# Moving every second block's h from row to time order with VectorE turns and SBUF copies, in a state-space kernel on Trainium2

## The chip, the cores and the metric

The kernel runs on one core of a Trainium2 chip, as one launch. The metric is device time in microseconds (us) from start to end of the launch. Engines are named as in the profile: PE is TensorE, DVE is VectorE, ACT is ScalarE, POOL is GpSimd, SP is SyncE, whose queue issues all of this kernel's transfers.

## What is computed

The input x has 1024 tokens of 512 values. It is normalized by rows (xn), and the output is x plus two branches of xn. Cut to what matters:

```
# branch 1: a state-space layer, here 128 heads of 64, 8 groups, state size 128, chunks of 128 tokens
gate, hBC, dt = split(xn @ in_proj_w.T)            # 8192, 10240 and 128 columns
hBC = silu(causal_conv4(hBC))                      # h: 8192, B: 1024, C: 1024 columns
dt  = clip(softplus(dt + dt_bias), 0, 100);  A_cum = cumsum over a chunk of dt * -exp(A_log)
xch = h * dt                                       # per head and token
Y_diag = (C B^T * exp(segsum)) @ xch               # inside a chunk
states = B^T (decay * xch), carried over chunks    # across chunks
Y = Y_diag + (C @ previous state) * exp(A_cum) + h * D
out1 = groupnorm(Y * silu(gate)) * norm_w @ out_proj_w.T
# branch 2: xn @ base_W.T plus low-rank experts, top 2 of 8 by a router
```

## The kernel before

**Tiles.** Channels are cut into blocks of 128. A block of h holds two heads: 128 channels in the partitions, 1024 tokens along the row. There are 64 h blocks, 64 gate blocks, 8 blocks of B and 8 of C (one per group). The eight chunks are called z. Float32 products are made from a high and a low part of each operand, three matmuls in place of one.

**One block** (`block`, from L729). Its weights are loaded (wr), split into high and low parts by ACT and POOL (L391, L392), multiplied on PE in two halves of 512 tokens (pp_r, L491), and taken out of PSUM: a gate block by one ACT operation per half (L743), an h, B or C block by ACT (L750) and three DVE taps of the convolution (L759), then one silu on ACT (L762).

**One step of the scan** (`scan`) handles two h blocks, so four heads; there are 32 steps, u = 0 to 31. Four mask tiles L are loaded as broadcast rows of acum_d and made into exp(-relu(.)) by ACT (L840, L842), and multiplied by the group's C B^T on DVE (L844). Then h, which has channels in its partitions, must get tokens into its partitions: PE transposes it chunk by chunk into PSUM (L818, eight 128x128 transposes per block, in two sets of four), and DVE multiplies each set by dt on its way out (xdt, L867). POOL weights xdt by the decay (xf, L873) and takes the low part (L880); PE makes chunk states from it (ps, L891), DVE carries them (st, L898 and L902). PE makes the two parts of the output (yo, L926, and y, L937, both 64 columns at a time, in halves of the array), DVE and POOL add and gate them (L929, L941, L944, L947), and the block is stored to g_d. A loop over groups with the output projection follows (po, L1010).

**The group's B** needs the same exchange. For it `turn` exists: DVE transposes all 32x32 squares of the block in one instruction (L779), which puts the right values into squares that stand in the wrong partitions; four stores (L778) write them to a DRAM buffer turn_d in another order, and one load (MB) brings them back. ACT and DVE then split B into high and low parts (L798, L800). A constant, TURNED, says whether blocks of h take this way too: with 0, as here, none does (`aside` is then false), with 2 every second one.

**The order.** Nothing is issued in the order in which it is written. Every operation is recorded with an engine, an assumed duration, the buffers it reads and writes, and an urgency (the table URGE, plus a shift per step and kind in SHIFT). A planner then plays the five engines forward in time and, whenever an engine is free, takes the ready operation with the lowest urgency, within limits on buffers of each kind (CAPS) and a charge for changing between kinds of matmul (TURN) or activation tables. The result is one fixed list of instructions per engine. Each engine works through its own list in order; an instruction that waits holds up all behind it on the same engine, SP's transfers included.

Of the kernel before, what the change touches and what calls it, by code (L numbers as in the profile page):

```python
# [49 lines left out]
URGE = dict(w=13.332, part=1.468, proj=-0.321, evac=-1.263, silu=-2.207, group=-1.454, hT=0.733, xdt=4.109,  # L50
            xf=-2.187, split=-0.021, ps=-5.287, st=-1.748, Ll=-4.271, Lr=7.668, Le=-0.828, Lm=10.124, el=-2.727,
            yo=-1.239, tt=-8.284, y=2.439, yt=-5.971, out=3.035, switch=3.602, c0=52.272, c=0.059, ffn=33.567,
            rt=-6.333, la=-1.718, early=-6.258, hold=0.271, gate=0.323, w0=100.494, SL=0.902, SH=0.088, SM=-4.419,
            LS=-0.037, LH=-0.076, LM=0.521, HS=3.572, HL=3.045, HM=-4.925, MS=-0.425, ML=-0.865, MH=0.797,
            hold2=-0.366, late=0.054, late2=0.096)
CAPS = dict(hs=5, gate=12, ct=2, L=7, e=3, xdt=9, turned=8, moved=3, wr=3, wh=9, wl=3, y=3, tt=2, xf=2, mm=16, ts=11, yy=8)

SHIFT = {}
for what, rows in dict(
        Le={1: 0.47, 2: -0.26, 3: -1.05, 4: -0.15, 5: 2, 6: -0.49, 7: 0.27, 9: -0.05, 12: -1.87, 13: 1.14, 14: 0.19,  # L60
            15: 0.82, 16: 0.61, 17: 0.64, 18: 0.12, 19: 1.35, 20: -0.65, 21: 0.59, 22: 0.59, 23: 0.11, 24: 0.26,
            26: 3.27, 27: 0.06, 28: 0.68, 29: -0.13, 30: 0.62, 31: 2.11},
        Ll={0: -0.81, 1: 1.29, 2: -0.45, 3: -0.27, 4: 0.34, 5: 1.51, 6: 0.55, 8: -0.1, 9: -3.54, 10: 0.17, 13: -2.75,
            14: 0.07, 15: 1.23, 16: -0.51, 19: 0.31, 21: 1.11, 23: 0.35, 24: -0.27, 26: -1.24, 27: -0.09, 28: 0.23,
            29: 1.87, 30: 2.91, 31: 1.26},
        Lm={1: -0.01, 3: 0.04, 4: -3.35, 5: 0.23, 6: 0.13, 8: -0.27, 9: 2.6, 10: -1.27, 11: 0.6, 15: -0.14, 16: 1.77,
            17: -0.48, 18: -3, 19: 0.19, 21: 0.05, 22: 0.04, 24: -0.04, 25: -1.05, 26: 0.09, 27: -1.02, 29: 2.34,
            30: -0.67},
        Lr={0: -0.03, 5: -0.35, 6: 0.1, 7: 0.58, 8: 0.8, 9: 0.35, 10: 0.01, 11: 0.64, 12: -0.05, 13: 0.15, 14: -0.03,
            15: 0.13, 17: -0.16, 18: 0.47, 19: -0.38, 22: -0.94, 23: 0.63, 25: 0.03, 26: 0.42, 27: 0.08, 28: 0.06,  # L70
            30: 0.07},
        el={0: -0.13, 1: -0.13, 4: 0.19, 8: 0.01, 9: -0.05, 10: 0.85, 11: -0.34, 12: 0.69, 13: 1.01, 17: 1.18,
            21: -0.42, 23: -0.65, 24: -0.88, 26: -0.39, 27: 0.31, 28: -0.01, 29: -0.41, 30: -0.51, 31: -1.96},
        gate={1: -0.11, 2: 0.17, 4: -2.2, 7: 0.08, 8: 0.03, 9: -0.25, 10: -0.2, 11: 0.88, 12: 0.1, 13: 0.52,
            15: -1.48, 17: 0.24, 18: -0.36, 20: -0.68, 21: -0.62, 22: -0.12, 24: -0.17, 25: -0.55, 26: 0.1,
            27: -0.59, 28: 1.26, 30: -0.35, 31: 0.23},
        group={0: 0.08, 2: -0.39, 3: 0.43, 5: -2.97, 6: 1.03, 7: -2.93, 10: -0.48, 11: 0.11, 12: -0.47, 13: -0.13,
            15: -1.26, 16: 0.08, 17: 0.15, 18: -0.31, 19: 0.47, 20: 0.01, 21: 0.14, 22: -1.25, 23: -0.61, 24: 0.03,
            25: -1.26, 26: 0.04, 27: -0.01, 28: -0.98, 29: 1.81, 30: -0.02},
        h={0: 0.22, 2: -0.03, 3: 0.11, 4: -0.06, 5: 0.19, 7: 0.02, 8: -0.07, 11: 0.48, 12: 0.22, 15: 0.26, 16: 0.32,  # L80
            18: -0.06, 20: -0.81, 21: 0.45, 22: -0.08, 24: -0.07, 25: -0.04, 27: 0.79, 28: 0.3, 29: 0.32, 31: 0.34},
        hT={0: 0.48, 1: 0.55, 3: -0.04, 4: 0.37, 6: -0.13, 8: 0.36, 9: 0.02, 10: -0.05, 11: 0.01, 12: -0.06,
            13: 0.21, 14: -0.11, 17: -4.33, 18: 0.18, 20: -2.06, 21: -1.02, 22: -0.17, 23: -0.65, 24: -0.09,
            25: 0.12, 28: 0.23, 30: -0.09, 31: -0.09},
        out={0: 0.06, 1: 0.58, 2: -0.1, 3: -0.33, 4: 0.66, 5: -0.97, 6: 0.57, 9: -0.06, 10: -0.56, 11: -0.59,
            12: -0.03, 13: -0.36, 14: 0.66, 15: 0.02, 16: 3.94, 18: 0.13, 19: 0.24, 22: 2.65, 23: -0.26, 24: 0.58,
            25: 0.09, 26: -0.03, 27: 0.6, 28: 0.8, 30: 0.18, 31: 0.82},
        ps={0: -0.19, 1: 0.04, 2: -0.24, 3: -0.19, 4: -2.42, 5: -0.69, 7: 4.13, 8: -0.01, 9: 0.27, 10: 0.44,
            12: 1.55, 14: -0.11, 16: -0.83, 19: 0.38, 20: -0.04, 22: 0.86, 25: -0.16, 28: -0.18, 30: 0.94, 31: -0.26},
        split={0: 0.69, 1: 2.29, 3: -0.09, 4: -0.05, 5: -1.39, 7: -1.51, 8: 0.12, 9: -0.12, 10: -0.34, 11: 0.11,  # L90
            12: 3.76, 14: -0.07, 15: 1.18, 17: -0.36, 18: 0.76, 20: -0.21, 21: 0.97, 22: -0.02, 23: -0.1, 24: -0.72,
            25: 1.26, 26: 1.68, 27: 0.02, 28: -0.28, 30: 0.66, 31: -0.4},
        st={0: -0.77, 2: -0.11, 3: 2.97, 4: 0.09, 5: -1.75, 6: 1.37, 8: -0.2, 9: -0.16, 10: -0.19, 11: -1.63,
            12: -0.01, 13: 0.17, 17: -2.04, 21: -1.34, 22: -0.12, 23: -0.74, 24: 0.82, 25: 1.04, 26: 0.02, 27: 0.28,
            28: -0.04, 29: 0.76, 30: -5},
        tt={0: 0.8, 1: 0.82, 2: 1.2, 3: -0.51, 4: -0.89, 5: 0.08, 6: -0.29, 7: -0.12, 8: 0.03, 10: -2.95, 11: 0.49,
            12: 0.35, 13: 1.11, 14: 0.25, 15: -0.03, 16: 0.52, 18: 1.56, 21: 0.03, 22: 0.7, 23: -0.66, 24: 1.74,
            26: 0.42, 27: -1.68, 28: 0.86, 31: -0.69},
        xdt={1: 0.04, 2: 0.59, 3: -0.11, 4: -1.62, 6: 0.48, 7: -0.02, 10: 0.28, 11: 0.12, 12: 0.65, 14: 0.23,
            15: -0.14, 16: 0.62, 17: -0.88, 18: -0.44, 19: -0.92, 20: -0.18, 21: -0.39, 22: -0.44, 25: -0.4,  # L100
            27: -0.96, 28: -3.62, 30: -0.03},
        xf={0: 0.18, 1: 0.11, 2: 0.25, 3: 1.29, 4: -0.1, 5: 0.65, 6: -0.05, 7: 0.52, 10: -0.16, 11: -0.98, 12: -1.46,
            13: -0.66, 14: 1.03, 15: -1.06, 16: 0.12, 18: 1.8, 19: -0.08, 20: -0.27, 21: 0.04, 22: -0.14, 23: -0.26,
            24: -1.59, 25: -0.15, 26: 0.23, 28: -1.22, 30: 0.35},
        y={0: 0.4, 1: -0.78, 2: -0.58, 3: 0.78, 4: 0.26, 5: -2.28, 8: -0.51, 9: -0.08, 10: 0.01, 11: -0.93,
            12: -0.05, 13: 0.37, 15: -0.75, 16: -0.1, 17: 0.35, 18: -0.03, 19: 0.2, 21: -0.65, 22: -0.16, 24: -0.73,
            26: -0.01, 27: -0.2, 28: -0.1, 30: 0.15, 31: 0.17},
        yo={0: -0.42, 1: -0.12, 2: -0.02, 5: 0.15, 6: -0.84, 10: 0.52, 11: 0.52, 12: -0.34, 13: 0.23, 15: -0.73,
            16: 0.52, 17: 0.33, 18: -0.6, 19: -1.53, 20: 1.18, 23: 0.02, 25: 1, 27: -0.46, 31: 0.02},
        yt={0: -1.42, 1: 0.96, 3: -1.19, 5: 0.1, 6: -0.03, 7: 0.63, 8: -0.17, 9: -0.63, 10: -1.86, 11: -0.23,  # L110
            12: -0.77, 13: 0.99, 14: -0.18, 17: -0.08, 18: 1.77, 19: 0.17, 20: -2.08, 22: 1.6, 25: -2.21, 26: 0.48,
            28: -0.7, 30: -1.5, 31: -0.01}).items():
    SHIFT |= {(u, what): by for u, by in rows.items()}
LAND = 1.15
TURNED = 0
# [186 lines left out]
def block_kernel(ctx, tc, x, in_w, conv_w, conv_b, dt_bias, A_log, Dv, norm_w, out_w,  # L302
# [31 lines left out]
    turn_d = [dram.tile([4, 32, 4, 256], F32, name=f"turn_d{i}") for i in range(4)]  # L334
# [27 lines left out]
    def thing(name):  # L362
        return pl.buf(None, name)
# [19 lines left out]
    TURN_D = [thing(f"turn_d{i}") for i in range(4)]  # L383
# [387 lines left out]
    def turn(src, name, at, urge):  # L771


        turned, moved = new("turned", f"T{name}"), new("moved", f"M{name}")

        def store():
            for q in range(4):
                sp.dma_start(turn_d[at][q].rearrange("r i f -> i r f"), turned()[:, 256 * q:256 * q + 256])  # L778
        op("DVE", 1.17, lambda: dve.transpose(  # L779
            turned().rearrange("p (q z c) -> p z q c", q=4, z=NZ), src().rearrange("p (z q r) -> p z q r", q=4, z=NZ)),  # L780
            r=[src], w=[turned], urge=urge)
        op("SP", 2.3, store, lag=LAND * 9.4, r=[turned], w=[TURN_D[at]], urge=urge)
        dma(lambda: moved().rearrange("p (i f) -> p i f", i=4), lambda: turn_d[at].rearrange("q r i f -> (q r) i f"),
            4.4, r=[TURN_D[at]], w=[moved], urge=urge)
        return moved
# [35 lines left out]
    def scan(u, hs, gate):  # L821
        g, gr = u // 4, groups[u // 4]

        def at(what):
            return u + URGE[what] + SHIFT.get((u, what), 0.0)
# [274 lines left out]
```

## Time and profile before

| what | value |
| --- | --- |
| median of 3 runs | 1593.33 us (1593.29 to 1593.93) |
| the profiled execution | 1591.37 us |
| its span, first to last instruction | 1589.6 us |
| transposes of h on PE (L818) | x512, 62.8 us busy, 272 ns each (median) |
| multiplication by dt on DVE (L867) | x128, 84.0 us busy, 682 ns mean |
| turns of B on DVE (L779) | x8, 9.9 us busy, 1239 ns mean |
| stores of turned B (L778) | x32, 128 KB each; loads of it x8, 512 KB each |
| ACT table loads | 109.1 (L842), 59.0 (L743) and 55.2 us (L762) |
| transfers on the SP queue | 236.76 MB, 48.7% of the 16 engines' span |

A profile row names the line, engine, operation, output and inputs, then count, busy time, mean duration of one, and the engine's idle time just before such instructions with what ended it. Matmuls overlap in the array, so the mean duration of one is longer than the distance between two starts. A row of the timeline has the start and length in us. A row of waits says which instruction waited for which, us in total, how often, and the longest.

### The profile page before, as it was taken

What the parts mean: (1) busy time and instruction counts of PE and PEld (TensorE: products, weight loads), DVE (VectorE), ACT (ScalarE), POOL (GpSimd) and SP (SyncE); (2) the same over time, 40 slices, a digit from 0 to 9 for tenths busy, and PEclk for the clock granted to TensorE, in tenths of its full rate; (3) what the DMA queues carried; (4) which work ended last, traced back from release to release, by engine and by line L of the source; (5) the groups of instructions that cost most, each with busy time, mean ns of one, the idle gap of its engine ahead of it and who ended that gap; (6) DMA issues with size and microseconds to landing.
All of it is one profiled execution on the core that took longest, in us unless ns stands there. A gap on an engine that the chain in (4) does not pass through costs nothing.

```text
span 1589.6 us, 28731 instructions
## 1 busy us (share of the span) xinstructions
PE 1579.8 (99%) x10498; PEld 1341.6 (84%) x10498; DVE 1311.4 (82%) x2237; ACT 1265.0 (80%) x2244; POOL 853.5 (54%) x768
## 2 busy tenths in 40 slices
PE   9999999999999999999999999999999999999999
PEld 8888888888888888888888888888877888888887
DVE  7799788887887969977978887888778888989785
ACT  6999988997989899997998998989883555545432
POOL 3288578676766875877767756869665000000000
PEclk9999999999999999999999999999999999999999
DMA  4636346543465354363453543644635556545532
GB/s 133 233 104 213 112 138 204 170 159 122 146 177 155 131 187 150 124 183 117 153 166 126 187 154 126 182 161 143 174 108 181 146 146 173 146 121 153 140 88 72
DMA packets 156061, 238.59 MB, mean 150 GB/s; under 512 B 21392, under 2 KB 91152, under 8 KB 155920
## 3 DMA queue, kind: packets, MB, share of 16 engines
q1 hardware_dynamic: 155920, 236.76, 48.7%
q8 instruction: 83, 1.36, 0.4%
q14 instruction: 58, 0.48, 0.1%
HBM read 195.70 MB, written 41.01 MB: 149 GB/s over the span
## 4 chain that ended last, share of the span: by engine, by line
PE 84%; ACT 10%; DMA 2%; issue 1%; DVE 1%; POOL 1%; SPq 0%; ACTq 0%; POOLq 0%
PE pp_r L491 39%; PE po L1010 22%; PE y L937 6%; PE yo L926 6%; PE ps L891 4%; PE hT L818 3%; ACT L L840 3%; PE pf L717 1%; ACT L842 1%; ACT L L842 1%; ACT L743 1%; ACT g L743 1%; PE cb L810 1%; ACT wh L391 1%; DMA e<-exp_d 1%
## 5 line engine op out<-in xcount | busy, mean ns | idle before, releaser
L491 PE MATMUL pp_r<-xh,wh 128*128 128x512 f32 x1144 | 454.5, 397 | 0.0
L491 PE MATMUL pp_r<-xl,wh 128*128 128x512 f32 x1144 | 446.6, 390 | 0.0
L491 PE MATMUL pp_r<-xh,wl 128*128 128x512 f32 x1144 | 446.3, 390 | 0.3 <-POOL wl L392 0.3
L759 DVE SCALAR_TENSOR_TENSOR h<-pp_r,cw,h 128x512 f32<-128x512 f32 (+2 forms) x384 | 283.0, 746 | 50.7 <-ACT h L750 45.6
L840 ACT ACTIVATE L<-L,As 128x128 f32<-128x128 f32 x1024 | 318.6, 391 | 1.2 <-DMA L<-acum_d 1.2
L392 POOL TENSOR_TENSOR wl<-wr,wh 128x512 fp32r<-128x512 f32 x144 | 196.2, 1369 | 177.1 <-ACT wh L391 120.5
L844 DVE TENSOR_TENSOR L<-L,cbm 128x1024 f32<-128x1024 f32 x128 | 202.9, 1596 | 64.3 <-ACT L L842 63.1
L491 PEld LDWEIGHTS pp_r<-xh,wh 128*128 128x128 f32 x1144 | 214.9, 188 | 47.8 <-issue 5.3
L491 PEld LDWEIGHTS pp_r<-xh,wl 128*128 128x128 f32 x1144 | 214.7, 188 | 47.3 <-POOL wl L392 1.1
L491 PEld LDWEIGHTS pp_r<-xl,wh 128*128 128x128 f32 x1144 | 215.1, 188 | 40.8
L944 POOL TENSOR_TENSOR yt<-yt,tt 128x384 f32<-128x384 f32 (+1 forms) x128 | 166.3, 1308 | 78.5 <-DVE yt L941 67.1
L1000 ACT ACTIVATE gr<-gr 128x1024 f32<-128x1024 f32 x64 | 67.9, 1061 | 150.3 <-DVE gl L998 149.4
L947 POOL TENSOR_TENSOR g<-yt,g 128x512 f32<-128x512 f32 x128 | 181.8, 1427 | 1.9
L880 POOL TENSOR_TENSOR xdl<-xf,xdh 128x512 fp32r<-128x512 f32 (+1 forms) x128 | 161.3, 1268 | 34.0 <-ACT xdh L878 33.0
L902 DVE SCALAR_TENSOR_TENSOR st<-st,eA,ps 128x64 f32<-128x64 f32 x768 | 156.0, 275 | 2.3 <-PE ps L891 1.2
L873 POOL TENSOR_TENSOR xf<-xdt,dec 128x512 f32<-128x512 f32 (+1 forms) x128 | 135.0, 1063 | 38.0 <-DVE xdt L867 31.7
L1001 DVE TENSOR_REDUCE sq<-gr 128x128 f32<-128x1024 f32 x64 | 128.3, 2010 | 21.4 <-ACT gr L1000 21.4
L842 ACT ACTIVATE L<-L 128x1024 f32<-128x1024 f32 x128 | 135.4, 1058 | 1.3
L1010 PE MATMUL po<-owh,gh 128*128 128x512 f32 x512 | 127.2, 391 | 0.0
L1010 PE MATMUL po<-owh,gl 128*128 128x512 f32 x512 | 126.7, 389 | 0.0
L1010 PE MATMUL po<-owl,gh 128*128 128x512 f32 x512 | 126.5, 389 | 0.0
L937 PE MATMUL y<-L,xdt 128*64 128x128 f32 x2048 | 122.7, 273 | 0.0
(178 smaller groups left out, 2706.4 us busy)
## 6 DMA issues: line engine op xcount, KB each, us to landing
L<-acum_d SPq DMA_DIRECT2D x128, 512.0 KB
wr<-in_w SPq DMA_DIRECT2D x144, 256.0 KB
g_d<-g SPq DMA_DIRECT2D x64, 512.0 KB
gr<-g_d SPq DMA_DIRECT2D x64, 512.0 KB
e<-exp_d SPq DMA_DIRECT2D x128, 224.0 KB
ow<-out_w SPq DMA_DIRECT2D x64, 256.0 KB
turn_d<-TB SPq DMA_DIRECT2D x32, 128.0 KB
MB<-turn_d SPq DMA_DIRECT2D x8, 512.0 KB
```

What stands on the lines that cost most here:

```text
L392: op("POOL", dur[1], lambda: pool.tensor_tensor(lo(), raw(), f32(hi()), ALU.subtract), r=[raw, hi], w=[lo], urge=urge, port=True)
L491: pe.matmul(acc(), a[:, k, :], b[:, k, halves(half)], start=n == 0, stop=n == 11)
L759: dve.scalar_tensor_tensor(d, acc()[:, :n], cw[:, ci, k:k + 1], d, ALU.mult, ALU.add)
L840: act.activation(L()[:, z, :], L()[:, z, :], AF.Relu, bias=As()[:, z, h:h + 1], scale=-1.0)
L842: op("ACT", 0.97, lambda L=L: act.activation(L(), L(), AF.Exp, scale=-1.0), w=[L], urge=at("Le") + 0.05 * a, table="exp")
L844: op("DVE", 1.14, lambda L=L: dve.tensor_tensor(L(), L(), gr.cbm(), ALU.mult), r=[gr.cbm], w=[L], urge=at("Lm") + 0.05 * a, port=True)
L880: op("POOL", 1.24 if n == 4 else 0.96, lambda xf=xf, zs=zs, cols=cols: pool.tensor_tensor(xdl()[:, zs, cols], xf(), f32(xdh()[:, zs, cols] ...
L902: dve.scalar_tensor_tensor(st()[:, z, c], st()[:, z - 1, c], eA()[:, 4 * u + a, z:z + 1], pt()[:, z % 2, c], ALU.mult, ALU.add)
L937: pe.matmul(yp()[64 * a:64 * a + 64, zsl(z4)], xdt[j]()[:, z, 64 * a:64 * a + 64], M[2 * j + a]()[:, z, :], start=True, stop=True)
L944: op("POOL", 1.25 if n == 4 else 0.97, lambda yt=yt, tt=tt, part=part: pool.tensor_tensor(yt()[:, part], yt()[:, part], tt()[:, part], ALU ...
L947: op("POOL", 1.24, lambda yt=yt, j=j, hf=hf: pool.tensor_tensor(gate[j]()[:, halves(hf)], yt(), gate[j]()[:, halves(hf)], ALU.mult), r=[yt ...
L1010: pe.matmul(po(), a()[:, b, :], wts[g, b // per][k]()[:, b % per, :], start=n == 0, stop=n == 23)
```

## The change

Three things change.

- TURNED goes from 0 to 2: of the two h blocks in each step, the second no longer goes through PE. In its place stand one DVE turn, 16 transfers, and two DVE multiplications by dt that read SBUF (one per head, all eight chunks at once).
- `turn` no longer goes through DRAM. The turned block is copied straight from SBUF to SBUF, square column by square column: 16 transfers of 32 partitions x 256 elements (32 KB), recorded as four operations of four. B's blocks take this way too.
- URGE, CAPS and SHIFT get new values throughout, so all five lists of instructions differ.

```diff
-CAPS = dict(hs=5, gate=12, ct=2, L=7, e=3, xdt=9, turned=8, moved=3, wr=3, wh=9, wl=3, y=3, tt=2, xf=2, mm=16, ts=11, yy=8)
+CAPS = dict(hs=5, gate=22, ct=2, L=7, e=2, xdt=15, turned=6, moved=6, wr=3, wh=4, wl=19, y=7, tt=3, xf=2, mm=37, ts=14, yy=12)
...
-TURNED = 0
+TURNED = 2
...
-    def turn(src, name, at, urge):
+    def turn(src, name, urge):
...
-        def store():
-            for q in range(4):
-                sp.dma_start(turn_d[at][q].rearrange("r i f -> i r f"), turned()[:, 256 * q:256 * q + 256])
         op("DVE", 1.17, lambda: dve.transpose(
             turned().rearrange("p (q z c) -> p z q c", q=4, z=NZ), src().rearrange("p (z q r) -> p z q r", q=4, z=NZ)),
             r=[src], w=[turned], urge=urge)
-        op("SP", 2.3, store, lag=LAND * 9.4, r=[turned], w=[TURN_D[at]], urge=urge)
-        dma(lambda: moved().rearrange("p (i f) -> p i f", i=4), lambda: turn_d[at].rearrange("q r i f -> (q r) i f"),
-            4.4, r=[TURN_D[at]], w=[moved], urge=urge)
+        for q in range(4):
+            def move(q=q):
+                for i in range(4):
+                    sp.dma_start(moved()[32 * q:32 * q + 32, 256 * i:256 * i + 256],
+                                 turned()[32 * i:32 * i + 32, 256 * q:256 * q + 256])
+            op("SP", 1.85, move, lag=LAND * 4.9, r=[turned], w=[(moved, 1 << q)], urge=urge)
         return moved
...
-        moved = turn(gr.B, f"B{g}", g % 4, urge)
+        moved = turn(gr.B, f"B{g}", urge)
...
             if aside:
-                moved = turn(hs[j], f"h{b}", b % 4, at("hT"))
+                moved = turn(hs[j], f"h{b}", at("hT"))
```

The multiplication that a turned block takes is in the kernel before already, behind `if aside`: for each of the two heads it reads the moved tile and dt, and writes all eight chunks of that head's half of xdt.

## The prediction

> **What bounds the kernel now.** I read the page's first, second and fourth parts, then the busy times of one stage, then TensorE's own waits, then the timeline around one set of transposes.
>
> ```profile
> span 1589.6 us, 28731 instructions
> ...
> PE 1579.8 (99%) x10498; PEld 1341.6 (84%) x10498; DVE 1311.4 (82%) x2237; ACT 1265.0 (80%) x2244; POOL 853.5 (54%) x768
> ...
> PEclk9999999999999999999999999999999999999999
> ...
> PE 84%; ACT 10%; DMA 2%; issue 1%; DVE 1%; POOL 1%; SPq 0%; ACTq 0%; POOLq 0%
> ```
>
> TensorE is busy for all but 9.8 us of the span, at a clock that is granted in full, and the chain that ends last runs 84% through it. The h transposes stand almost wholly between 100 and 1200 us. The next line gives that stage: its length, busy time of PE, PEld, DVE, ACT and POOL, the clock, the DMA share.
>
> ```profile
> 100.00:1200.00 1100.00, 1096.83 (x8169) 940.70 (x8166) 911.55 (x1740) 1009.71 (x1891) 796.50 (x705) 1.00 0.49 154
> ```
>
> VectorE has 188 us idle here (1100 - 912), ScalarE 90. TensorE's own waits after the first 20 us are few; these are the longest three:
>
> ```profile
> PE ps L891 <- POOL xdl L880: 1.7, 1, 1.7
> ...
> PE hT L818 <- ACT h L762: 0.8, 3, 0.4
> PE cb L810 <- ACT C L762: 0.4, 1, 0.4
> ```
>
> So what TensorE no longer has to do comes off the end, as long as the others can feed it at the new pace.
>
> **What is taken away.** Of 512 transposes (L818) 256 go, 8 for each of 32 blocks. Sixteen of them, with the projections around them:
>
> ```profile
> 1147.10 0.40 PE L491 MATMUL pp_r<-xh,wl 128*128 128x512 f32 x1
> 1147.34 1.91 PE L818 MATMUL hT<-ident,h 128*128 128x128 f32 x16
> 1149.00 0.47 PE L491 MATMUL pp_r<-xh,wh 128*128 128x512 f32 x1
> 1149.31 0.39 PE L491 MATMUL pp_r<-xl,wh 128*128 128x512 f32 x1
> ```
>
> Matmuls overlap, so the pace is read from starts. From the first transpose to the projection behind them is 1.66 us, and that projection holds its successor off for 0.31 instead of the usual 0.23: 1.74 / 16 = 0.109 us each. 256 x 0.109 = 27.9 us. Both ends: the group's busy time (62.8 us for 512, which counts overlapped tails) would give 31.4; its share of the chain (2.9% of 1589.6 = 46) gives 23. I take 27.9.
>
> The Trainium skill, "TensorE: Matmul & The Clock Gate", Part 4, gives about 275 ns for a 128x128 transpose inside a kernel. The trace has 272 ns as duration of one, but a pace of 109; priced by the page the 256 would be worth 70 us and the result would be near 1525. The overlap decides, not the duration.
>
> **Order chosen anew, on TensorE.** Counting runs of one kind of matmul in the two instruction lists, the stretches of half-width products (yo and y, L926 and L937) go from 46 to 51. Entering one costs 0.32 instead of 0.23 us (starts at 1165.10 and 1165.42), and by the start times in the trace the first matmul behind one starts 0.20 us after the last, against 0.055 within it: 0.24 us each, 5 x 0.24 = +1.2. Nothing else on TensorE changes in number. Its work: -27.9 + 1.2 = -26.7.
>
> **VectorE gets more.** The block transpose exists for B:
>
> ```profile
> 174.09 1.24 DVE L779 STREAM_TRANSPOSE TB<-B 128x1024 f32<-128x1024 f32 x1
> 175.25 2.28 DVE L759 SCALAR_TENSOR_TENSOR h<-pp_r,cw,h 128x512 f32<-128x512 f32 x3
> ```
>
> Minimum, median and maximum in ns of the old multiplication by dt and of the mask product, each from the view of its line:
>
> ```profile
> L867 DVE TENSOR_TENSOR xdt<-hT,dts x128: 674/681/693, 80.6 to 1188.3; 128x512 f32<-128x512 f32 x128
> ```
> ```profile
> L844 DVE TENSOR_TENSOR L<-L,cbm x128: 1209/1492/2356, 65.2 to 1188.9; 128x1024 f32<-128x1024 f32 x128
> ```
>
> 32 x 1.16 (start to start) = 37 us. The 64 multiplications of these blocks (681 ns, hardly spread, one input in PSUM) now read SBUF twice, as L844 does, which is twice as wide and spreads: halved, 0.60, 0.75 or 1.18. So -5, +4 or +32 us; I take +4, the median. VectorE's stage goes from 912 to 953. The stage itself shrinks to 1100 - 27 = 1073, which leaves 120 us idle. Cover: that idle. If it were gone, each us would reach TensorE's end.
>
> **The copies and the wait they add.** 16 transfers of 32 x 256 elements per block, 640 in all with B's. No row shows an SBUF-to-SBUF transfer; two bracket it, each four issues from the same queue:
>
> ```profile
> 175.35 2.32 SPq L778 DMA_DIRECT2D turn_d<-TB  x4
> 177.78 1.03 SPq L388 DMA_DIRECT2D wr<-in_w  x2
> 184.21 0.33 SPq L388 DMA_DIRECT2D MB<-turn_d  x1
> ```
> ```profile
> 1308.73 1.74 SPq L1029 DMA_DIRECT2D sums_d<-sums  x4
> 1310.57 1.00 SPq L388 DMA_DIRECT2D gr<-g_d  x2
> 1311.75 1.38 SPq L388 DMA_DIRECT2D sums<-sums_d  x1
> ```
>
> In both, the last issue waits until the four before have landed. Low end (32 rows each, but tiny): 16 x 0.435 = 7.0 to issue, then 1.3, together 8.3 us. High end (rows of 1 KB, as here, but 128 of them): 16 x 0.58 = 9.3, then 6.5, together 15.8. I take 10, near the low end, because a new transfer has the 32 rows of the low row and a quarter of the high row's bytes.
>
> The waiting instruction is the multiplication on VectorE; behind it in order stand taps, states and masks for TensorE and POOL. From the new list I added up, by the paces above, VectorE's own work between each h transpose and its first multiplication: 3.9 to 29.8 us, median 12.9. With 10 us to land, 7 of 32 waits are not covered, 18.5 us of waiting in all; inside 120 us of idle. I charge TensorE +2 us for it. In return half of the 23.9 us that VectorE waited for TensorE's transposes should go; what is late next is POOL's xf (L873), which already waited 31.7 us for this multiplication.
>
> Edits that I cost at nothing: B's way (store, then load, 175.35 to 184.21 before the load even starts) gets shorter, and nothing on TensorE waited for it. 278 us of added issue on SP (640 x 0.435): behind each burst stand loads of weights, mask rows and e, but SP waits for buffers over 1000 us of the span, and ScalarE waited 1.2 us in all for mask rows, so loads are early; uncovered, a burst delays them by 7 us each time. The new buffer limits (e two instead of three, for one) act through the order alone. Added packets: 20480 of 1 KB at the 46 ns of B's old ones is 59 us of 16 engines, less 26 for what goes, on a share of 48.7%. PSUM banks come free. ScalarE keeps its 180 table loads.
>
> The Trainium skill, "DMA: Bandwidth & Descriptors", Rules for kernel authors, speaks against this change: transfers under 64 KB are mostly overhead and should be merged, and these have 32 KB. By the fit in its section on the anatomy of one DMA (made for the GpSimd path), about 2.0 us fixed each, a block's 16 would take 32 us one after the other and every wait would be late (an estimate). The four sums transfers overlapped, so I do not follow it.
>
> **Sum.** The profiled execution took 1591.37 us (span 1589.6). 1591.4 - 26.7 + 2 = 1566.7. The median of the runs, 1593.33, is 2.0 above the profiled one, so **1568.5**.
>
> **Rivals.**
> 1. ScalarE becomes a second bound. It is busy 1010 us of the stage; at 1073 it may idle 63, now it idles 90. Of that 50 us is waiting for TensorE's projections (31.6 and 18.8 in its waits), which speaks against. If 77 of the 90 stay, the stage is 1087 and half the gain is lost: about 1580 (1575 to 1588).
> 2. Slower: the landing. VectorE's work is 953; of its waits for ScalarE (63.1 for masks, 44.6 for taps) I let half, 55, remain. With landings at L us, the uncovered waits sum to 18 (L = 10), 72 (14), 109 (16). 953 + 55 + 91 = 1099 is the old stage: it decides from L = 15. At 16 the stage is 1117, 17 more: about 1610. For it: the high row, bursts behind 512 KB loads. Against: quarter-size transfers.
> 3. The transposes' time is filled by waits and nothing shows: 1593. TensorE's few waits speak against.
> 4. More comes off (31.4, no new stall, the old 3 us of waits gone): about 1559.
>
> **Chances.** Forecast (1560 to 1575) 0.57; rival 1 0.25; rival 2 0.10; rival 3 0.04; rival 4 0.04. Leaving out rivals 2 and 3 and the far end of 4, the range is 1559 to 1588. A difference of 0.2%, 3.2 us, is about what a measurement of this kernel can tell from none. Faster 0.86, same 0.04, slower 0.10.
>
> **What would show it.** Right: hT x256 with half the busy time, PE's busy time near 1550 and still 99%, VectorE near 1352, and VectorE's waits for the copies under 40 us. The landing is read from the first copy's issue to the multiplication that waited. Wrong: PE's idle above 20 us with h or xdt as releaser (rival 2), or waits on ScalarE's L and h lines (rival 1). The forecast fails if the copies land later than 15 us after the transpose, or if the new order loses TensorE more at its changes of kind than I counted.

## The result and the profile after

The kernel after takes 1629.03 us in the median of 4 runs (1628.28 to 1630.5), beside 1593.31 us (1591.7 to 1593.93, 4 runs) for the kernel before on the same chip. The ratio is 1.0227, with a 95% interval of 1.0215 to 1.0239. I had forecast 1568.5 us, in a range of 1559 to 1588: the change makes the kernel slower, and the time lies 41 us above the range. The profiled execution after took 1628.29 us.

The page of the kernel after, its rows on the span, the engines, TensorE's clock, the chain that ended last, and the new transfers (count, size of one, median us from issue to landing):

```profile
span 1626.6 us, 29055 instructions
...
PE 1575.5 (97%) x10242; PEld 1326.5 (82%) x10242; DVE 1348.2 (83%) x2269; ACT 1265.5 (78%) x2244; POOL 873.9 (54%) x768
...
PEclk9999999989999999999998999999999999999999
...
PE 55%; ACT 18%; DMA 9%; SPq 6%; DVE 6%; POOL 5%; issue 3%; DVEq 0%; ACTq 0%; POOLq 0%
...
Mh<-Th SPq DMA_DIRECT2D x512, 32.0 KB, 1.9
```

Three things differ from the rows of before. TensorE has 256 matmuls less but only 4 us less of busy time, and its idle time has grown from 9.8 to 51 us. Two slices of its clock row show an 8. In the chain, TensorE fell from 84% to 55%; transfers and SyncE's queue (SPq), together 2% before, now hold 15%. TensorE's time that was to come off the end has gone into waiting.

The same stage as before (100 to 1200 us), with PE, PEld, DVE, ACT and POOL busy, the clock and the DMA share:

```profile
100.00:1200.00 1100.00, 1061.42 (x7707) 902.97 (x7706) 922.37 (x1725) 986.39 (x1843) 791.16 (x675) 0.98 0.54 160
```

TensorE has 39 us idle here instead of 3, though VectorE (178 us idle) and ScalarE (114) both have room. No engine is the bound; something arrives late. The waits name it. First TensorE's own, then those of the other engines for transfers:

```profile
PE ps L891 <- POOL xdl L880: 13.3, 11, 2.5
PE hT L818 <- ACT h L762: 9.4, 3, 5.0
PE ps L891 <- ACT xdh L878: 8.1, 4, 3.8
PE pp_r L491 <- ACT wh L391: 8.0, 3, 7.2
```
```profile
ACT wh L391 <- DMA wr<-in_w: 31.5, 7, 10.4
...
DVE xdt L853 <- DMA Mh<-Th: 28.1, 9, 6.9
...
ACT L L840 <- DMA L<-acum_d: 20.1, 9, 5.4
```

TensorE waits for states (ps) and for weights (pp_r). Behind the first stand VectorE's 28.1 us of waiting for the copies and ScalarE's 20.1 us for mask rows (1.2 before); behind the second, ScalarE's 31.5 us for weight loads, for which it did not wait at all in the kernel before. (Which wait stands behind which is read from the order of the work; part of it is in the chain below.) The weights and the mask rows have nothing to do with the copies, except that all share SyncE's queue and the DMA engines.

The timeline of that queue around the longest stall:

```profile
307.58 1.16 SPq L388 DMA_DIRECT2D wr<-in_w  x1
309.30 8.43 SPq L782 DMA_DIRECT2D Mh<-Th  x12
317.83 1.18 SPq L388 DMA_DIRECT2D e<-exp_d  x2
319.05 2.49 SPq L782 DMA_DIRECT2D Mh<-Th  x4
...
325.67 2.24 SPq L388 DMA_DIRECT2D wr<-in_w  x2
...
328.95 2.73 SPq L388 DMA_DIRECT2D wr<-in_w  x2
332.62 12.28 SPq L782 DMA_DIRECT2D MB<-TB  x16
```

SyncE issues almost without a pause from 307 to 329 us (its longest wait there is 0.5 us), and 16 of these issues are copies; 16 more follow from 332.6 on. The weight load at 325.67 stands behind the first 16. The chain that ended last goes through it:

```profile
325.67 10.05 DMA wr<-in_w
...
335.80 0.64 ACT wh L391
...
336.56 1.29 POOL wl L392
...
337.90 2.50 PE pp_r L491 x5
```

The load lands only at 335.7, ScalarE and GpSimd split it, and TensorE, which had been out of weights since 329.3, goes on at 336.5 with the high parts and at 337.9 with the low ones. (This landing of 10 us is slow beside the median of 3.5: the loads and stores that had queued up went out close together, and in the second row below the DMA share is 1.00.) The place alone proves no cause: just ahead of this load, at 322.3, one of SyncE's issues also waited 0.1 us for ScalarE. Experiment 1 tells what it is like without the bursts: there TensorE has no pause above 1 us after the first 20 us.

What such a stall leaves behind is seen in four stretches of the same place, with the length, PE, PEld, DVE, ACT and POOL busy, the granted clock, DMA share and GB/s:

```profile
316.00:329.00 13.00, 13.00 (x63) 10.71 (x61) 12.25 (x17) 7.98 (x12) 9.90 (x8) 1.00 0.65 163
329.00:332.60 3.60, 0.26 (x2) 0.00 (x0) 3.47 (x5) 0.00 (x0) 0.00 (x0) 1.00 1.00 397
332.60:342.80 10.20, 6.12 (x15) 4.44 (x16) 0.00 (x0) 6.98 (x16) 4.08 (x4) 0.50 0.58 212
342.80:352.00 9.20, 9.20 (x106) 8.65 (x106) 7.37 (x14) 9.14 (x19) 7.50 (x10) 1.00 0.68 237
```

After 3.6 us almost without a matmul the granted clock is 0.50 for 10.2 us; the matmuls that run in it count as busy, at half pace. That is why TensorE's busy time hardly fell. In the whole run there are seven such stretches, 47.8 us long; in the kernel before there is none within the work.

So the profiled time, forecast at 1566.7 for this execution, came out 61.6 us higher. Summing the starts that come more than 250 ns later than a matmul's usual pace, TensorE's gaps grew from 10.6 us (20 of them) to 58.6 us (52 of them): 48 us. The rest, about 14 us, is near what the half clock should cost: TensorE is busy for 35.8 of those 47.8 us, projections start 0.43 us apart there instead of 0.23, and so this work takes some 17 us longer (an estimate).

### The profile page after: what moved, and what is told of

Its sections match the earlier page's. It is cut to its first block, busy times and chain, and to the rows that moved or that the text cites. A ratio compares the mean times of both kernels' runs of the same rounds, so it can differ in the third digit from the quotient of the medians.

```text
span 1626.6 us, 29055 instructions
## 1 busy us (share of the span) xinstructions
PE 1575.5 (97%) x10242; PEld 1326.5 (82%) x10242; DVE 1348.2 (83%) x2269; ACT 1265.5 (78%) x2244; POOL 873.9 (54%) x768
## 4 chain that ended last, share of the span: by engine, by line
PE 55%; ACT 18%; DMA 9%; SPq 6%; DVE 6%; POOL 5%; issue 3%; DVEq 0%; ACTq 0%; POOLq 0%
PE po L1010 21%; PE pp_r L491 19%; ACT L L840 5%; SPq L782 5%; PE y L937 4%; DMA L<-acum_d 4%; PE ps L891 3%; PE yo L926 3%; ACT L L842 2%; DMA wr<-in_w 2%; ACT L842 2%; DVE h L759 2%; POOL xdl L880 2%; PE pf L717 1%; ACT h L750 1%
## 5 line engine op out<-in xcount | busy, mean ns | idle before, releaser
L840 ACT ACTIVATE L<-L,As 128x128 f32<-128x128 f32 x1024 | 317.5, 391 | 20.1 <-DMA L<-acum_d 20.1
L844 DVE TENSOR_TENSOR L<-L,cbm 128x1024 f32<-128x1024 f32 x128 | 189.7, 1489 | 51.7 <-ACT L L842 51.2
L873 POOL TENSOR_TENSOR xf<-xdt,dec 128x512 f32<-128x512 f32 (+1 forms) x128 | 139.6, 1103 | 61.7 <-DVE xdt L853 32.7
```

Source lines behind the costliest of these rows:

```text
L840: act.activation(L()[:, z, :], L()[:, z, :], AF.Relu, bias=As()[:, z, h:h + 1], scale=-1.0)
L844: op("DVE", 1.14, lambda L=L: dve.tensor_tensor(L(), L(), gr.cbm(), ALU.mult), r=[gr.cbm], w=[L], urge=at("Lm") + 0.05 * a, port=True)
```

## The experiments

The theories were: that SyncE's queue, held by each burst of sixteen issues, is the loss (Q), either because the loads behind the burst are late (Q1) or because the multiplication's own last pieces are (Q2); that the planner was only told too low a price for the issues (P); that the newly chosen order of the work, with VectorE's added work, costs time wherever the copies go (D; for B's way alone it is called R); and that the copies themselves land late or crowd the DMA engines (L). The kernel before took 1591.4 to 1593.3 us beside these runs. Apart from runs 12 and 13 each time below is of one execution; four executions of the changed kernel lie within 2.2 us. "After" means the changed kernel. Gaps are those of TensorE, counted as above.

### 1. One transfer instead of sixteen

```diff
-                for i in range(4):
-                    sp.dma_start(moved()[32 * q:32 * q + 32, 256 * i:256 * i + 256],
-                                 turned()[32 * i:32 * i + 32, 256 * q:256 * q + 256])
+                if q == 0:
+                    sp.dma_start(moved(), turned())
```

> Leaves out: each turned tile is copied by one transfer of the whole 512 KB tile in place of 16 of 32 KB, so squares stay in the wrong partitions and the output is not the reference's; bytes, dependencies and the order on PE, DVE, ACT and POOL are those of the changed kernel. Theory Q (the issue queue: 16 issues of 0.635 us hold SP for 10.2 us per block, the loads behind them start late, TensorE runs dry and its clock halves after each longer gap): 0.4 us of issue per block, 1565 to 1580. Theory D (VectorE's 37 us more, and an order that leaves TensorE waiting wherever the copies go): 1615 or more. Theory L (the copies land late, or their bytes crowd the DMA engines): bytes unchanged and one transfer lands in 4 to 9 us, so 1595 to 1630.

Measured: **1566.36 us**, 62.7 below the changed kernel. The order on the four computing engines, the turns and the multiplications are the same in both; only SyncE's issues are fewer. Its page (the last row is 512 KB per copy, 3.2 us to land):

```profile
span 1564.6 us, 28300 instructions
...
PE 1554.0 (99%) x10242; PEld 1313.3 (84%) x10242; DVE 1353.1 (86%) x2269; ACT 1263.9 (81%) x2244; POOL 875.8 (56%) x768
...
Mh<-Th SPq DMA_DIRECT2D x32, 512.0 KB, 3.2
```

TensorE is at 99% again, its busy time is 25.8 us below that of before, its gaps are 22 with 11.6 us, and the clock is never halved within the work. The same bytes move, and one copy lands later than one small piece did. So neither the bytes, nor the new order, nor VectorE's added work is the loss: the number of issues is. (The packets differ too, 4 KB here and 1 KB in the changed kernel; run 13 has as many small ones.) Of the 62 us between the two spans 40.5 are idle time of TensorE and 21.5 busy time.

### 2. Four transfers

```diff
-                for i in range(4):
-                    sp.dma_start(moved()[32 * q:32 * q + 32, 256 * i:256 * i + 256],
-                                 turned()[32 * i:32 * i + 32, 256 * q:256 * q + 256])
+                sp.dma_start(moved()[32 * q:32 * q + 32, :], turned()[32 * (3 - q):32 * (3 - q) + 32, :])
```

> Leaves out: four transfers of 32 x 1024 (128 KB) in place of 16, values in wrong places, the order on the four compute engines unchanged. Q: 2.5 us of issue per block instead of 10.2, so about a quarter of the loss stays: 1570 to 1590. D: 1615 or more. L: as with one copy, 1595 to 1630.

Measured: **1570.85 us**, gaps of 14.6 us. From 1 to 4 issues per tile costs 4.5 us, from 4 to 16 costs 58. The price of an issue is not constant; that fits a burst which costs only where it is longer than what the loads behind it have in hand.

### 3. The bursts alone, in the kernel before

```diff
+    def burst(src):
+        for i in range(4):
+            for q in range(4):
+                sp.dma_start(spare[32 * q:32 * q + 32, 256 * (i % 2):256 * (i % 2) + 256],
+                             src()[32 * i:32 * i + 32, 256 * q:256 * q + 256])
...
+        if extra:
+            burst(src)
```

> The kernel before with 16 transfers of 32 KB per second block, from h to a tile that nobody reads, put into SP's queue where the block's transposes are recorded; all four compute lists are those of before and TensorE keeps its 512 transposes. Q: late loads alone must hurt: 1615 to 1655. D: within 5 us of before. L as lateness of the copies themselves: nothing waits for them, within 5 us; L as crowding of the DMA engines: 1598 to 1610.

Measured: **1607.17 us**, 14.2 above before, gaps of 22.6 us and three stretches of half clock. No one needs these copies, so the bursts slow this kernel without any late data of their own. The time lies below the range for the queue (1615 to 1655) and inside the one for crowding of the DMA engines (1598 to 1610), so this run does not tell those two apart; run 13 does. The 32 bursts cost 0.44 us each here, where 40 cost 1.6 each in the changed kernel. In the order of before the loads stand earlier: 18 weight loads and 31 mask rows lie ready for less than a burst's 10.2 us before their use, against 32 and 39 in experiment 1, which has the changed order and no bursts.

### 4. B's new way alone, and 7, the same with one copy

```diff
-TURNED = 2
+TURNED = 0
```

> The kernel before with B's new way alone (8 blocks, 16 copies each, no trip through DRAM), TURNED 0, urgencies and limits of before; the planner reorders a little. Q: 8 bursts of 10 us, 1594 to 1606. D and L: within 4 us of before.

> The run with B's new way alone, again with the urgencies of before, and the order on the four compute engines as in that run, but one whole-tile transfer in place of B's 16; values in wrong places. Q: the eight bursts were the loss, 1592 to 1600. Theory R (the loss there came from the reordering): 1610 to 1620.

Both keep URGE, CAPS and SHIFT of before and change only `turn`; the second has the single transfer of experiment 1. Measured: **1618.21 us** with 16 copies per block of B (25 above before), **1606.37 us** with one. Both miss their ranges: the first lies above the 1594 to 1606 for the bursts alone, the second between its two. Twelve of the 25 are the eight bursts. The other 13 come without any burst: the planner, given other costs for B's way, issues a different order from the same urgencies (TensorE's list differs in a third of its places), and that order is what remains to explain them. An order chosen for one set of costs is worth 13 us less with another, which speaks for choosing it anew after an edit, as the change does.

Under the label of experiment 12 this second kernel, by a mistake of mine, ran again in place of the one that its expectation describes. It gave 1604.93 us, a ratio of 1.0072 (1.005 to 1.0094) to the kernel before, so the 13 us are no accident of one run. The expectation, which is about the kernel of experiment 8, is answered by run 13:

> The complete version through device memory with the four loads straight behind the store (five issues in place of sixteen), the best complete one so far, timed against the kernel before in several rounds. If its one look of 1581.3 holds, the ratio lies at 0.9925, its interval within 0.991 to 0.994, and it is truly faster than the kernel before. If that look was a lucky one, the ratio comes out above 0.996.

### 5 and 9. Own pieces early, neighbours still late

The diff is that of run 9; in run 5 a region of the spare place was written again two copies later, in run 9 eight later.

```diff
+                if q == 0:
+                    sp.dma_start(moved(), turned())
+                for i in range(q == 0, 4):
+                    k = turns[0] % 8
+                    turns[0] += 1
+                    sp.dma_start(spare[32 * (k % 4):32 * (k % 4) + 32, 256 * (k // 4):256 * (k // 4) + 256],
+                                 turned()[32 * i:32 * i + 32, 256 * q:256 * q + 256])
```

> The changed kernel with one whole-tile transfer first, which the multiplication reads, and 15 of the 16 small transfers behind it, into a spare tile that nobody reads; values in wrong places, order on the four compute engines unchanged. It parts theory Q in two. Q1, SP is held and the loads of other operations (weights, mask rows, e) come late: 1612 or more. Q2, the multiplication itself waits for its sixteenth copy: its data land some 3 us after the turn, so 1566 to 1580.

Measured: 1773.4 us, far beyond what either theory had in mind. Its spare regions were written again so soon that copies waited for earlier ones (SyncE's waits for them sum to 236 us), and SyncE was held much longer than meant. The run says nothing on the split. Experiment 9 repeats it with eight regions in turn:

> One whole-tile copy that the multiplication reads, then 15 of the small copies to a spare place that nobody reads, with each region of the spare place written again only after eight further copies. It leaves out the rearranging of the pieces, so the output is not the reference's. The order on the four computing engines is that of the changed kernel; SyncE issues 16 transfers per turned tile as there, but the data that the multiplication needs is the first of them to land. Theory Q1, the queue held by the burst makes the loads behind it late: the time stays near that of the changed kernel, 1605 to 1635, with TensorE's gaps above 40 us in sum. Theory Q2, the multiplication's own pieces come too late because the last of 16 is issued 10 us after the first: the time falls to 1566 to 1580, that of the single copy. A time between 1580 and 1605 shares the loss out between the two.

Measured: **1614.31 us**, with 51.8 us of gaps, in the bounds of Q1. With the multiplication's data issued first, 48 of the 62.7 us remain. TensorE's waits and the other engines' waits for loads are those of the changed kernel; VectorE's wait ahead of the multiplication is smaller, but not gone:

```profile
PE ps L896 <- POOL xdl L885: 13.8, 12, 2.8
PE pp_r L491 <- ACT wh L391: 8.1, 2, 7.8
```
```profile
ACT wh L391 <- DMA wr<-in_w: 30.9, 7, 11.0
ACT L L845 <- DMA L<-acum_d: 17.9, 9, 3.6
DVE xdt L858 <- DMA spare<-Th: 12.4, 4, 5.3
```

30.9 against 31.5 us for weights, 17.9 against 20.1 for mask rows. In the last row the run does not do all that it was meant to: in these four cases the multiplication started only when the last copy to the spare place had landed, although its own data had landed 6 to 20 us before. So the 14.7 us that went with 15.7 us of VectorE's waiting are the least that the own pieces cost, and 48 us the most that the neighbours' delay does.

### 6. The planner told the price

```diff
-            op("SP", 1.85, move, lag=LAND * 4.9, r=[turned], w=[(moved, 1 << q)], urge=urge)
+            op("SP", 2.54, move, lag=LAND * 4.9, r=[turned], w=[(moved, 1 << q)], urge=urge)
```

> The changed kernel, complete, with the planner told 2.54 us in place of 1.85 for four issues, urgencies and limits as they are. If only the price was missing (theory P), the new order puts loads ahead of bursts and most comes back: 1570 to 1600. If 10 us of issue per block cannot be placed with these urgencies, or any new order loses what these were tuned to: 1605 or more.

Measured: **1630.42 us**, gaps of 57.4 us, 47.8 us at half clock, as in the changed kernel. Theory P finds no support: with 2.54 us for four issues (the 0.635 us measured for one) and the same urgencies the planner arranges things no better. Urgencies chosen anew with this price were not tried.

### 8 and 13. The exchange through DRAM, with five issues

```diff
+                if q == 0:
+                    sp.dma_start(turn_d[n].rearrange("i r q f -> (i r) (q f)"), turned())
+                if q == 3:
+                    for p in range(4):
+                        sp.dma_start(moved()[32 * p:32 * p + 32].rearrange("r (i f) -> r i f", i=4),
+                                     turn_d[n][:, :, p, :].rearrange("i r f -> r i f"))
```

This version is complete and keeps the changed kernel's order on the four computing engines.

> Complete: the changed kernel with its order on the four compute engines, but each turned tile goes out by one store of 512 KB to DRAM and comes back by four loads of 32 partitions. SP issues 5 instead of 16 and waits some 3 us for the store in between, about 6 us per block. Q by the amount of SP time (0.5 us gave 1566, 2.5 gave 1571, 10.2 gave 1629): 1575 to 1600. D: 1615 or more.

> The complete version through device memory with the four loads straight behind the store, five issues in place of sixteen, timed against the kernel before in several rounds. If its one look of 1581.3 holds, the ratio lies at 0.9925 with an interval inside 0.990 to 0.995. If that look was a lucky one, the ratio comes out above 0.996.

Measured: 1581.28 us in run 8, then, in run 13, **1580.08 us** in the median of 4 runs (1577.45 to 1581.4), a ratio of **0.9924 (0.9907 to 0.994)** to the kernel before. It moves each byte twice and is still 49 us faster than the changed kernel, and 12.9 us faster than the kernel before. The timed run's page and what SyncE waited for:

```profile
span 1575.7 us, 28541 instructions
...
PE 1557.9 (99%) x10242; PEld 1315.4 (83%) x10242; DVE 1353.8 (86%) x2269; ACT 1264.6 (80%) x2244; POOL 875.0 (56%) x768
```
```profile
SPq L789 <- DMA turn_d<-Th: 69.6, 22, 7.1
SPq L789 <- DMA turn_d<-TB: 26.8, 8, 6.3
```

The loads may not start before the store has landed, so SyncE stands for 96 us in all. I took this for the 14 us that separate the version from the single copy.

The run also settles the crowding that run 3 left open. The row of SyncE's queue (packets, MB, share of the 16 DMA engines' span) in the changed kernel and in this one:

```profile
q1 hardware_dynamic: 181264, 249.38, 51.7%
```
```profile
q1 hardware_dynamic: 179344, 270.33, 56.7%
```

Both move 20480 packets of 1 KB. Weights land in 3.5 and 3.7 us (medians), mask rows in 6.7 and 6.5. The DMA engines have no less to do, and with 5 issues per tile in place of 16 the time is 49 us lower: crowding is not the main loss.

### 10 and 11. The loads later

The four loads are put off until two (run 10) or four (run 11) further issues of SyncE have gone out, or until something needs them.

```diff
+                if q == 3:
+                    pend.append([2, loads, (turned, moved)])
...
+        for p in list(pend):
+            p[0] -= o.eng == "SP"
+            if p[0] < 0 or any(b in o.frees for b in p[2]) or any(
+                    b.kind.pool is m.kind.pool and b.slot == m.slot for b in o.takes for m in p[2]):
+                p[1]()
+                pend.remove(p)
```

> The way through device memory (one store of the whole tile, four loads), complete, with the four loads issued two further issues of SyncE later, so that other loads go out while the store lands. The order on the four computing engines stays that of the changed kernel. The run with the loads straight behind the store took 1581.3 with 100 us of SyncE's waiting for the stores. If that holding of the queue is what is left over the single copy's 1566.4, SyncE's wait for the stores falls below 50 us and the time to 1568 to 1576. If the later loads only move the wait to the multiplication on VectorE (5.0 us there so far), that wait rises above 15 us and the time stays at 1578 to 1590.

> As the run before it, with the four loads four issues of SyncE later instead of two. If the holding of the queue is what counts: within 4 us of the run with two, SyncE's wait for the stores below 25 us. If the multiplication's wait takes over: above the run with two by more than 4 us, with VectorE's wait for the loads over 20 us.

Measured: **1594.01** and **1634.97 us**. SyncE's waits for the stores did fall, from 100 to 24 and then 4 us, and the time rose: my expectation that the queue would gain by it was wrong, since the rival named there, the multiplication's own wait, took over; run 10 lies above that rival's range (1578 to 1590) too. VectorE's waits for its data went from 5.0 us to these, in runs 10 and 11:

```profile
DVE xdt L863 <- DMA Mh<-turn_d: 29.3, 12, 5.9
```
```profile
DVE xdt L863 <- DMA Mh<-turn_d: 78.8, 19, 6.7
```

24 us more of waiting cost 12.7 us, 74 more cost 53.7: half to three quarters of the wait reaches the end, the half clock after longer pauses included.

### 14. One copy, but late

Experiment 1 with its single transfer put off by up to four issues, so that no burst exists and only the own data are late.

```diff
+                if q == 0:
+                    pend.append([4, lambda: sp.dma_start(moved(), turned()), (turned, moved)])
```

> As the run with one whole-tile copy in place of 16 (which leaves out the rearranging of the pieces), only that this copy is issued four other issues of SyncE later, or straight ahead of its first reader if that comes before. SyncE's queue is held by nothing more than one issue per tile, so no other load can be late through a burst: what is measured is the price of late own data alone. If VectorE's idle time covers such waits, as the prediction had it (18.5 us of waiting for 2 us), the time is 1566 to 1570 with 20 us or more of VectorE's waits for the copies. If late own data reach TensorE at about half their sum, as the later loads through device memory suggest, the time is 1566 plus half of VectorE's waits, 1576 to 1620.

Measured: **1600.07 us**, 33.7 above experiment 1.

```profile
DVE xdt L853 <- DMA Mh<-Th: 34.2, 10, 7.1
...
ACT wh L391 <- DMA wr<-in_w: 7.5, 3, 4.5
```

Weights are hardly late. VectorE waits 34.2 us, and ScalarE and GpSimd 16.3 us more for copies that landed late. A price of a tenth, as I had it, is refuted; per us of all these waits it is 0.67, per us of VectorE's alone 0.99.

## Why the prediction was wrong

**What bounds the kernel, and what is taken away: right.** Experiment 1 is the change without its many issues. It took 1566.4 us, where I had forecast 1568.5 for the whole. There TensorE's busy time is 25.8 us lower than before (my terms: -26.7), the transposes are x256 with 33.4 us, about half, and the gaps stay at 11.6 us.

**VectorE's work: right in the sum, in part by luck.** +37 and +4 us gave 1352; measured 1353.1 in experiment 1, 1348.2 in the changed kernel. The multiplication that reads SBUF, bounded between 0.60 and 1.18 us and taken at 0.75, has a median of 0.69, but spreads so far that its mean is 0.92:

```profile
L853 DVE TENSOR_TENSOR xdt<-Mh,dts x64: 649/693/1819, 94.9 to 1221.1; 128x512 f32<-128x512 f32 x64
```

In experiment 1 these 64 take 57.3 us, 15 more than half of the old 84.0, where I had 4, and the 32 turns take 39.6, where I had 37. The mask product, for which I had no change, takes 195.4 us instead of 202.9, and smaller changes make up the rest.

**The issues, priced too low.** I bracketed one between 0.435 and 0.58 us and took the low end, since the tiny sums transfers also had 32 rows. The trace has, in ns (least, median, most):

```profile
L782 SPq DMA_DIRECT2D Mh<-Th x512: 507/589/1937, 82.4 to 1208.4; - x171
```

With the steps between, one takes 0.635 us of the queue and sixteen 10.2, not 7.0: the row of B's old stores, which has the same width of 1 KB, was the nearer one. The landing of one piece was no trouble: 1.87 us behind its issue in the median. The last piece lands 12.2 us after the first issue in the median, inside my 8.3 to 15.8, but up to 22.6 us after it, since the sixteen issues, with others between them, took up to 21.3 us.

**The step that failed: "loads are early; uncovered, a burst delays them by 7 us each time", costed at nothing.** My ground was that SP waits for buffers over 1000 us of the span and ScalarE waited only 1.2 us for mask rows. Neither shows how early. The trace does, if the n-th landing is paired with the n-th use. In the kernel before, weights lie ready for 20.2 us in the median and mask rows for 15.3; but 18 of 144 weight loads and 31 of 128 mask rows have less than 10.2 us in hand. In the changed kernel these counts are 52 and 49. A queue that waits for a buffer is not idle in the sense of having time to spare: it issues the load in the moment in which it can, and what is queued ahead of it then is paid by the load. Experiment 9 prices this at 48 us at most. If the 12.4 us for which VectorE still waited there cost half to all of their length, as in runs 10, 11 and 14, 36 to 42 us are left for it (an estimate). Experiments 1, 2 and 8 confirm it from the other side: with 1, 4 and 5 issues per tile the time is 1566, 1571 and 1580 us.

**The second failure: VectorE's idle time as cover.** I expected 7 of 32 waits to be uncovered, 18.5 us, and charged 2 us. The waits came somewhat larger than expected (9 times, 28.1 us, below my limit of 40), but they are not free: runs 10, 11 and 14 price each us of them at half to a whole us. VectorE's idle time does not cover them; behind the waiting multiplication stand states, masks and taps, and POOL's chain to the next ps, so I take it that the idle time lies elsewhere in the stage. In the changed kernel this is worth at least the 14.7 us between it and experiment 9.

**What neither step had: the clock.** Every idle stretch of TensorE of 1.9 us or more in the changed kernel was followed by 3.4, 6.8 or 10.2 us at half clock, none of 1.6 us or less was. The Trainium skill, "TensorE: Matmul & The Clock Gate", Part 1, says that the clock is set by windows of 3.413 us, half after an idle one and full after a busy one. The lengths agree (one, two and three windows); a full idle window was not needed, since 1.9 us were enough. The other runs show that the length of a pause alone does not decide: 2.12 us in run 2 and 2.35 us in run 9 were followed by no half clock. In every run that has more than one such change the moments at which the clock changed lie whole multiples of 3.413 us apart. If the traces are cut at these moments into windows, those two pauses leave at most 1.59 and 1.21 us idle in any one window; over all runs, after their first 15 us, a window at full clock with more than 1.9 us idle was always followed by half clock, and one with less than 1.6 us never, except for one stretch each in runs 5 and 8 that came after a window without idle time. Between the two figures both occur.

**The rivals.** Rival 2 named the slower side, by late landing, from 15 us on. From the turn's end to the last piece it took 13.1 us in the median, but over 15 us in 14 of 32 blocks, which was one of my signs of failing. Its path, VectorE's stage filling up, was not reached, for VectorE keeps 178 us idle; the late pieces cost all the same, about a quarter of the 62.7 us or more. The main mechanism, the neighbours' delay, stood in my text as an edit that costs nothing, and not as a rival. Rival 1 (ScalarE), 3 and 4 find no support: experiment 1 has TensorE at 99%.

**The rule that I set aside.** The Trainium skill, "DMA: Bandwidth & Descriptors", Rules for kernel authors, would have merged these transfers. I rejected it because its reason, the overhead of each transfer, would not add up when transfers overlap, and in that I was right: the pieces overlapped and landed fast. The rule still pointed the right way, for the time that the issuing queue takes. On that the page, in Issuing engines are not separate DMA queues, says that the time to initiate a transfer is usually small relative to the transfer itself. Here it was 0.59 us beside 1.87 to land, and with sixteen in a row, 10.2 us, it was the larger of the two.

**What stays open.** Whether the bursts would do no harm from another engine's queue was not tried, nor urgencies chosen with the right price of an issue. The loss is divided between the neighbours' delay and the own pieces only within the bounds above. The 14 us between the exchange through DRAM and the single copy are not divided either: SyncE's waits for the stores may hold part of them, but runs 10 and 11, which took those waits away, made the data late instead.

## What to carry to other kernels

When a change adds transfers, price them first as time on the issuing queue (count times the spacing of issues), and ask of the loads behind them how long each lay ready before its use: the loads with the least in hand, not the median or the summed waits, say what a burst costs. An idle engine covers a wait only where its idle time stands, so a wait on an in-order engine ahead of TensorE's operands counts at half its length or more until a run shows otherwise. Where a rearrangement needs many small pieces, a way with fewer issues can win although it moves the bytes twice.

## What the runs showed of the hardware

- Issuing one copy from SBUF to SBUF took SyncE 0.49 us for a whole tile of 512 KB (experiment 1) and 0.59 us for a piece of 32 KB (changed kernel), both medians; a plain weight load of 256 KB took as little as 0.33 us. Small pieces are not cheaper to issue.
- A whole 512 KB tile copied from SBUF to SBUF landed in 3.2 us (experiment 1), a 32 KB piece in 1.9 (changed kernel), both medians.
- TensorE's clock was halved for whole multiples of 3.41 us, on a grid that is fixed within a run, after windows of that length with more than 1.9 us idle; in the changed kernel this held for 47.8 us. A pause of 2.35 us that fell across two windows (run 9) was followed by none.
